# Router in column halves, half of batch 1's convolution on TensorE, and a new order up to routing

## Chip, cores and metric

One core of a Trainium2 chip. The metric is the device time of one execution in microseconds (us). All times below are us unless they say ns.

## What is computed

The input x has 8 batches of 512 tokens with 1024 channels. Each token is convolved along its batch, a router picks one of 8 experts for it, and that expert's 1024 x 1024 matrix is applied. The result is added to x. All of it is float32.

```
y = depthwise causal conv1d(x, taps of cond_2048, K = 8 taps, per channel) + b
idx = argmax_e(y . w_router[e])          # E = 8 experts, one for each token
out = x + w_experts[idx] @ y
```

Tokens are sorted by expert into tiles of 128 rows; 35 tiles have rows, of at most 39 (`NS`).

## The kernel before, in words

**Channels and chunks.** The 1024 channels are 8 chunks (`c`) of 128 partitions. Four chunks are one half (`h`). A unit `u = (b, j0, nj)` is a run of `nj` blocks of 128 tokens of batch `b`. All batches are one unit of four blocks, except batch 2, which is cut in two (`early` is the first of them, (2, 0, 2)), because the list `STAGES` (L37) has a stage that ends after 10 blocks.

**Convolution on VectorE.** One step convolves two chunks of a unit. `first_taps` (L203) makes tap 0 with the bias on ScalarE into a tile of the ring `acc` (three buffers, each one half of a unit); `other_taps` (L220) adds seven taps on VectorE, 14 instructions a step. `begin` (L278) lets ScalarE be up to three steps ahead, as far as `acc` has room.

**Convolution on TensorE.** `spread_taps(c)` (L310) makes eight 128 x 128 diagonal matrices of the taps of a chunk on ScalarE, in slot 0 of the weight buffer `w_all`; `conv_on_pe` (L315) multiplies the shifted rows by them and adds up in PSUM. Before, this is done for chunks 0 to 5 of the early unit.

**Outs.** `conv_out` (L242), here called an out, turns 128 tokens of one half back to rows: four transposes on TensorE into PSUM (`pc`), a copy on ScalarE into `rt`, and after the last block of the unit one DMA on ScalarE's queue to `conv_rows` in DRAM. Only then is the `acc` buffer free.

**Router.** The convolution is linear, so `router_batch` (L352) multiplies x itself by taps times router weights: 64 columns (8 taps x 8 experts), 8 chunks accumulated in PSUM. ScalarE copies the result, a DMA writes it to `z_rows` in DRAM, and SP's queue reads it back shifted by tap into `zs`; `router_logits` (L373) adds the taps by a matmul with `sel`. Batches 0 and 1 are in `xp`, batches 2 to 7 in the three slots of `w_all`, loaded at the start.

**Routing.** L419 to L633 is a chain of small instructions, nearly all on VectorE, with a few matmuls: argmax (`best`, `chosen`), counts by expert (`ps_tot`, `upto`), the place of each token, and last `tok_gather`, `tile_info` and `tile_count`.

**Tiles.** Stage m of `STAGES` says that the first m blocks of 128 tokens are convolved. Each stage makes full tiles for every expert that has 128 rows left, and `last_stage(t)` (L43) is the stage by which tile t surely exists. `fetch(t)` (L706) gathers a tile's rows from `conv_rows` and x on GpSimd's queue; `turn` (L711) transposes them (`cxT`); `multiply` (L724) does 32 passes of 512 columns into `y_ring`; `add_x` (L737) adds x on VectorE; `finish_tile` scatters. `load(t)` (L684) reads an expert's 4.2 MB into one of three slots of `w_all`, in two DMAs on SP's queue, if the expert changes. The slot is a register value. For dependencies, `weights` (L668) treats it as slot `t % 3`. The load of tile 1 waits for the gather of tile 0.

**Order.** The schedule is by hand: what is written first stands first in an engine's queue. Up to routing the order is that of L390 to L406. After it a planner (L753 to L835) keeps two clocks, `now["pe"]` and `now["conv"]`: 1.75 for two chunks of a tile, 0.5 for an out or a turn, 9.4 or 5.4 for a convolution step, 0.7 for an `add_x`, and 14.0 (`LAND`) from a fetch to its turn. It puts a step, an out or a turn where its clock says that it is due. A tile is fetched when `2 * last_stage(t)` outs are written and it is at most two tiles ahead. `load_conv_x(b + 2)` stands where the last step of batch b is.

Of the kernel before, what the change touches and what calls it, by code (L numbers as in the profile page):

```python
# [33 lines left out]
KE = K * E  # L34


STAGES = (8, 10, 12, 16, 20, 24, 32)  # L37
W = len(STAGES)
R = W * E
U = 40  # L40
# [14 lines left out]
def conv_then_routed_ffn(  # L55
# [58 lines left out]
    def iota(shape, pattern, base, channel, name, dtype=F32):  # L114
        t = rc.tile(shape, dtype, name=name)
        nc.gpsimd.iota(
            t,
            pattern=pattern,
            base=base,
            channel_multiplier=channel,  # L120
            allow_small_or_imprecise_dtypes=True,
        )
        return t
# [12 lines left out]
        wr_sb.unsqueeze(2).to_broadcast([P, NC, K, E]),  # L136
        ALU.mult,
    )
    lbw = zp.tile([P, NC, KE], F32, name="lbw")
    nc.vector.memset(lbw, 0.0)  # L140
    nc.vector.tensor_copy(lbw[:, :, KE - E :], wr_sb)

    col = iota([P, P], [[1, P]], 0, 0, "col")
    row = iota([P, 1], [[1, 1]], 0, 1, "row")
# [2 lines left out]
    nc.vector.tensor_tensor(rowu, rowu, row, ALU.add)  # L147
    falling = iota([P, E], [[-1, E]], E, 0, "falling")
    high = iota([P, NT], [[P, NT]], -BIG, 0, "high")
    sel_i = iota([KE, E], [[-1, E]], KE, 1, "sel_i", I32)  # L150
    nc.vector.tensor_single_scalar(sel_i, sel_i, E - 1, op=ALU.bitwise_and)
    sel_f = rc.tile([KE, E], F32, name="sel_f")
    nc.vector.tensor_copy(sel_f, sel_i)
    sel = rc.tile([KE, E], F32, name="sel")
    nc.vector.tensor_single_scalar(sel, sel_f, 0.0, op=ALU.is_equal)
    ones = rc.tile([P, P], BF16, name="ones")
    nc.vector.memset(ones, 1.0)
    notbelow = rc.tile([P, P], BF16, name="notbelow")
# [31 lines left out]
    def operands(u, c):  # L190
# [9 lines left out]

        return acc, shifted

    def first_taps(u, c):  # L203

        b, j0, nj = u
        if c % HC == 0:
            acc_of[u, c // HC] = accp.tile(
                [P, HC, nj * P], F32, tag="acc", name=f"acc_{b}_{j0}_{c // HC}"
            )
        acc, shifted = operands(u, c)  # L210
        for i in (c, c + 1):
            nc.scalar.activation(  # L212
                acc(i),
                shifted(i, 0),
                AF.Identity,
                bias=bias_sb[:, i : i + 1],
                scale=taps_sb[:, i, 0:1],
            )
# [23 lines left out]
    def conv_out(u, h, j):  # L242
# [13 lines left out]
            nc.scalar.dma_start(to.rearrange("(j p) d -> p j d", p=P), rt_of[u, h])  # L256


    ON_PE = 6
    early = next(u for u in units if u[0] == 2)  # L260
    steps = [
        (u, c) for u in units for c in range(0, NC, 2) if u != early or c >= ON_PE
    ]
    now = {"conv": 12.0}
    outs = []
# [12 lines left out]
    def begin():  # L278

        while steps and len(begun) < 3:  # L280
            u, c = steps[0]
            full = [key for key in acc_of if key not in drained]
            if c % HC == 0 and (len(full) >= 3 or u[0] not in xp_of):
                return
            if c % HC and (u, c // HC) not in acc_of:
                return
            first_taps(u, c)
            begun.append(steps.pop(0))
# [3 lines left out]
    def next_step():  # L292
        begin()
        u, c = begun.pop(0)
        other_taps(u, c)
        now["conv"] += 9.4 if u[2] == TB else 5.4
        if c % HC == HC - 2:
            outs.extend((now["conv"] + 1.0, u, c // HC, j) for j in range(u[2]))
        if c == NC - 2 and u[1] + u[2] == TB and u[0] + 2 < B:
            load_conv_x(u[0] + 2, 1)  # L300
        begin()

    def more_steps():
        return bool(steps or begun)

    diag_of = w_all[:, 0].rearrange("p c f -> p (c f)").rearrange(
        "p (c k q) -> p c k q", k=K, q=P
    )

    def spread_taps(c):  # L310

        for k in range(K):
            nc.scalar.mul(diag_of[:, c, k, :], ident, taps_sb[:, c, k : k + 1])

    def conv_on_pe(u, c):  # L315
        b, j0, nj = u
        n = nj * P
        if c % HC == 0:
            acc_of[u, c // HC] = accp.tile(
                [P, HC, n], F32, tag="acc", name=f"acc_{b}_{j0}_{c // HC}"  # L320
            )
        acc, shifted = operands(u, c)
        pc = ps.tile([P, n], F32, tag="pc", name=f"pcv_{b}_{j0}_{c}")
        for k in range(K):
            nc.tensor.matmul(  # L325
                pc, lhsT=diag_of[:, c, k, :], rhs=shifted(c, k), start=(k == 0), stop=(k == K - 1)
            )
        nc.scalar.activation(acc(c), pc, AF.Identity, bias=bias_sb[:, c : c + 1], scale=1.0)
        if c % HC == HC - 1:
            outs.extend((now["conv"], u, c // HC, j) for j in range(nj))  # L330

    ps_lb = psr.tile([KE, 1], F32, tag="pt", name="ps_lb")
    for c in range(NC):
        nc.tensor.matmul(
            ps_lb, lhsT=lbw[:, c, :], rhs=bias_sb[:, c : c + 1], start=(c == 0), stop=(c == NC - 1)
        )
    lb = const.tile([KE, 1], F32, name="lb")
    nc.scalar.copy(lb, ps_lb)  # L340

    lg = psr.tile([P, NT, E], F32, tag="y", name="lg")
# [2 lines left out]
    zs_of = {}  # L345
    zbs = []
    for i in range(2):
        zb = zp.tile([KE, ZL], F32, name=f"zb_{i}")
        nc.gpsimd.memset(zb, 0.0)
        zbs.append(zb)  # L350

    def router_batch(b):  # L352
        pz = ps.tile([KE, S], F32, tag="pc", name=f"pz_{b}")
        for c in range(NC):
            nc.tensor.matmul(  # L355
                pz,
                lhsT=wrt[:, c].rearrange("p k e -> p (k e)"),
                rhs=x_of[b][:, c, :],
                start=(c == 0),
                stop=(c == NC - 1),  # L360
            )
        zb = zbs[b % 2]
        nc.scalar.activation(zb[:, K - 1 : K - 1 + S], pz, AF.Identity, bias=lb, scale=1.0)
        nc.scalar.dma_start(z_rows[b], zb)

        zs = zp.tile([KE, S], F32, tag="zs", name=f"zs_{b}", bufs=B)
        z = z_rows[b]
        nc.sync.dma_start(
            zs, bass.AP(z.tensor, z.offset, [[E * ZL + 1, K], [ZL, E], [1, S]])
        )  # L370
        zs_of[b] = zs

    def router_logits(b):  # L373
        for j in range(TB):
            nc.tensor.matmul(
                lg[:, b * TB + j, :],
                lhsT=zs_of[b][:, j * P : (j + 1) * P],
                rhs=sel,
                start=True,
                stop=True,  # L380
            )

    def some_outs(n):
        for _ in range(n):
            next_out()

    def before_early():
        return steps[0][0] != early or bool(begun)

    for b in range(B):  # L390
        while now["conv"] < 14.0 + 7.0 * b and before_early():
            next_step()
        router_batch(b)
        if b >= 4:
            for c in range(2 * (b - 4), min(2 * (b - 3), ON_PE)):
                spread_taps(c)
        if b == B - 2:
            some_outs(TB)
    for i in range(B - 1):
        router_logits(i)  # L400
    while before_early():
        next_step()
    some_outs(TB)
    router_logits(B - 1)
    some_outs(TB)
    conv_on_pe(early, 0)  # L406
    zp_cm.__exit__(None, None, None)
    rp_cm = tc.tile_pool(name="route", bufs=1)
    rp = rp_cm.__enter__()
# [26 lines left out]
    ps_rank = psr.tile([P, E, NT], F32, tag="pt", name="ps_rank")  # L436
    nc.tensor.matmul(ps_tot, lhsT=ones, rhs=chosen, start=True, stop=True)
    nc.tensor.matmul(ps_rank, lhsT=notbelow, rhs=chosen, start=True, stop=True)
    some_outs(TB)
    conv_on_pe(early, 1)  # L440
    conv_on_pe(early, 2)


    upto = new([P, E, NT], "upto")
# [79 lines left out]
    for q in range(4):  # L524
        ts = slice(q * QT, (q + 1) * QT)
        nc.vector.tensor_tensor(
            in_row[:, ts, :],
            colb.unsqueeze(1).to_broadcast([P, QT, P]),
            part[:, 0, ts].unsqueeze(2).to_broadcast([P, QT, P]),
            ALU.is_equal,  # L530
        )
        for t in range(q * QT, (q + 1) * QT):
            nc.tensor.matmul(
                ps_tok,
                lhsT=in_tile[:, t].rearrange("p a u -> p (a u)"),
                rhs=in_row[:, t],
                start=(t == 0),
                stop=(t == NT - 1),
            )
# [39 lines left out]
    perm = new([P, NS], "perm")  # L579
    nc.vector.tensor_scalar(perm, col[:, :NS], to, None, ALU.is_equal)  # L580

    tok_u = new([2 * U, P], "tok_u")
    nc.vector.tensor_copy(tok_u, ps_tok)
    ps_perm = psr.tile([P, NS], F32, tag="pt", name="ps_perm")
# [46 lines left out]
    nc.vector.tensor_copy(tile_info, info_f[:NS, :])  # L631
    nc.vector.tensor_copy(tok_scatter, tok_f)
    nc.vector.tensor_copy(tile_count, end_run[0:1, W - 1, E - 1 :])  # L633
    for c in range(3, ON_PE):
        conv_on_pe(early, c)
    rp_cm.__exit__(None, None, None)
    psr_cm.__exit__(None, None, None)
    rc_cm.__exit__(None, None, None)
# [29 lines left out]
    def weights(t, slot, *at):  # L668

        a = w_all[(slice(None), ds(slot, 1), *at)]
        fixed = w_all[(slice(None), slice(t % WB, t % WB + 1), *at)]
        return bass.AP(
            a.tensor,
            a.offset,
            a.ap,
            runtime_checks=a.runtime_checks,  # L680
            dep_tracking_offset=fixed.offset,
        )
# [69 lines left out]

    STEP, OUT, LAND = 1.75, 0.5, 14.0  # L753
    now["conv"] += 20.0
    now["pe"] = now["conv"] - 4.0
    ready = {}

    def fetch_ready():
# [9 lines left out]
    def load_ready():  # L768
        ahead = 3 if state["fetched"] else 1
        while state["loaded"] < NS and state["loaded"] < state["tile"] + ahead:  # L770
            load(state["loaded"])
            state["loaded"] += 1

    def try_out():
        if outs and outs[0][0] <= now["pe"]:
# [108 lines left out]
```

## Time and profile before

| | us |
|---|---|
| median of 3 runs (lowest, highest) | 724.84 (724.02, 725.93) |
| the profiled execution | 729.59 |
| its span, first to last instruction | 727.8 |
| TensorE busy in the span | 655.6 |
| VectorE busy | 354.8 |
| ScalarE busy | 147.8 |
| mean granted TensorE clock | 0.951 |

PE is TensorE's matmul, PEld its weight load, DVE is VectorE, ACT is ScalarE, POOL is GpSimd, SP is SyncE; a q after the name means its DMA queue. A row of the timeline has start, length, engine, line, operation, `out<-in`, shape, count, and in brackets how long the engine had been idle and what ended that. Lines are those of the kernel before. DMA queue q1 is the loads of SP, q10 the writes of ScalarE, q0 the gathers and scatters of GpSimd.

### The profile page before, as it was taken

How to read it: one execution, taken by the hardware profiler on the slowest of the kernel's cores; microseconds unless marked ns; L12 is line 12 of the kernel's file. 1: busy time of each engine (PE TensorE's matmuls, PEld its weight loads, DVE VectorE, ACT ScalarE, POOL GpSimd, SP SyncE). 2: the span in 40 equal slices, each digit the busy share in tenths (PEclk: the TensorE clock that was granted, in tenths of full speed). 3: DMA queues.
4: the chain of work that ended last, by engine and by line, in shares of the span. 5: the costliest groups of instructions: out<-in, count | busy, mean ns of one | idle time of the engine just before them, and what ended most of it. 6: DMA issues, size and time to landing. Idle time of an engine off the chain costs nothing. (4 is left out here: it accounts for less than half of the span.)

```text
span 727.8 us, 6970 instructions
## 1 busy us (share of the span) xinstructions
PE 655.6 (90%) x2005; PEld 326.8 (45%) x2005; DVE 354.8 (49%) x610; ACT 147.8 (20%) x266; POOL 110.6 (15%) x131
## 2 busy tenths in 40 slices
PE   6997988679697799899999979999999999999990
PEld 2332866334353455355545434444444444444440
DVE  6997871999799298998990000101010101010100
ACT  4256221522321232233111000000000000000000
POOL 1000001020202211211212023112212221122110
PEclk9998898899899799999999998999999999999996
DMA  8992265989899999799999999998473567296320
GB/s 320 426 357 100 71 234 206 368 285 406 304 425 402 386 402 365 284 427 426 421 426 414 406 377 347 405 374 317 165 301 129 191 262 294 87 381 255 118 88 8
DMA packets 42838, 217.63 MB, mean 299 GB/s; under 512 B 4144, under 2 KB 4144, under 8 KB 35120
## 3 DMA queue, kind: packets, MB, share of 16 engines
q1 hardware_dynamic: 17984, 143.73, 49.4%
q0 software_dynamic: 15696, 55.58, 20.6%
q10 hardware_dynamic: 9120, 17.84, 6.6%
q8 instruction: 20, 0.33, 0.2%
q14 instruction: 18, 0.15, 0.1%
HBM read 224.46 MB, written 36.19 MB: 358 GB/s over the span
## 5 line engine op out<-in xcount | busy, mean ns | idle before, releaser
L729 PE MATMUL y<-w_all,cxT 128*128 x1120 | 506.2, 601 | 5.5 <-DVE xr L739 4.8
L729 PEld LDWEIGHTS y<-w_all,cxT 128*128 128x128 f32 x1120 | 208.1, 193 | 231.8 <-issue 222.7
L231 DVE SCALAR_TENSOR_TENSOR sum<-xp,taps_sb,sum 128x512 f32<-128x512 f32 (+1 forms) x330 | 206.8, 706 | 0.0
L739 DVE TENSOR_TENSOR xr<-y,xr 128x512 f32<-128x512 f32 x70 | 47.9, 688 | 325.9 <-PE y L729 325.9
L716 ACT COPY cxT<-pt 128x512 f32<-128x512 f32 x72 | 42.1, 586 | 357.5 <-PE pt L715 356.4
L715 PE MATMUL pt<-ident,cx 128*128 128x128 f32 x288 | 46.3, 289 | 26.0 <-DMA cx<-conv_rows,tok_gather 26.0
L252 ACT COPY rt<-pc 128x512 f32<-128x512 f32 x64 | 37.1, 585 | 129.1 <-PE pc L247 129.1
L715 PEld LDWEIGHTS pt<-ident,cx 128*128 128x128 f32 x288 | 37.7, 149 | 56.1 <-DMA cx<-conv_rows,tok_gather 28.2
L660 POOL DMA_INDIRECT xr<-in_x,tok_gather x37 | 35.2, 953 | 181.0 <-DMA out<-xr,tok_scatter 176.7
L660 POOL DMA_INDIRECT cx<-conv_rows,tok_gather x37 | 35.8, 968 | 166.0 <-DMA conv_rows<-rt 93.2
L743 POOL DMA_INDIRECT out<-xr,tok_scatter x35 | 36.0, 1029 | 150.4 <-DVE xr L739 134.4
L231 DVE SCALAR_TENSOR_TENSOR sum<-xp,taps_sb,acc 128x512 f32<-128x512 f32 (+1 forms) x66 | 44.1, 711 | 20.9 <-ACT acc L212 20.9
L247 PE MATMUL pc<-ident,acc 128*128 128x128 f32 x256 | 41.5, 293 | 12.5 <-DVE acc L231 6.7
L247 PEld LDWEIGHTS pc<-ident,acc 128*128 128x128 f32 x256 | 33.1, 150 | 39.8 <-issue 24.2
L212 ACT ACTIVATE acc<-xp,bias_sb,taps_sb 128x512 f32<-128x512 f32 (+1 forms) x66 | 46.9, 772 | 6.4 <-ACT rt L252 2.9
L231 DVE SCALAR_TENSOR_TENSOR acc<-xp,taps_sb,sum 128x512 f32<-128x512 f32 (+1 forms) x66 | 43.4, 698 | 0.0
L355 PE MATMUL pz<-w_all,wrt 128*64 128x512 f32 x96 | 42.9, 608 | 0.0
L355 PEld LDWEIGHTS pz<-w_all,wrt 128*64 128x64 f32 x96 | 13.4, 141 | 28.8 <-issue 28.2
L325 PE MATMUL pcv<-xp,w_all 128*128 128x256 f32 x96 | 24.4, 417 | 0.3 <-issue 0.2
L325 PEld LDWEIGHTS pcv<-xp,w_all 128*128 128x128 f32 x96 | 20.0, 211 | 5.8 <-issue 2.2
L92 POOL MEMSET xp<- 128x64 f32 x8 | 1.2, 156 | 104.6 <-DVE acc L231 104.3
L355 PE MATMUL pz<-xp,wrt 128*64 128x512 f32 x32 | 15.4, 642 | 1.3 <-DMA xp<-in_xT 1.3
(106 smaller groups left out, 83.4 us busy)
## 6 DMA issues: line engine op xcount, KB each, us to landing
w_all<-in_w_experts SPq DMA_DIRECT2D x74, 2048.0 KB
xp<-in_xT SPq DMA_DIRECT2D x7, 2048.0 KB
conv_rows<-rt ACTq DMA_DIRECT2D x14, 1024.0 KB
w_all<-in_xT SPq DMA_DIRECT2D x6, 2048.0 KB
xp<-in_xT SPq DMA_DIRECT2D x2, 1024.0 KB
conv_rows<-rt ACTq DMA_DIRECT2D x4, 512.0 KB
z_rows<-zb ACTq DMA_DIRECT2D x8, 130.0 KB
zs<-z_rows SPq DMA_DIRECT2D x8, 128.0 KB
```

Source lines behind the costliest of these rows:

```text
L212: nc.scalar.activation(acc(i), shifted(i, 0), AF.Identity, bias=bias_sb[:, i : i + 1], scale=taps_sb[:, i, 0:1],)
L231: nc.vector.scalar_tensor_tensor(acc(i) if k == K - 1 else sums[i - c], shifted(i, k), taps_sb[:, i, k : k + 1], acc(i) if k == 1 else sum ...
L247: nc.tensor.transpose(pc[:, c * P : (c + 1) * P], acc_of[u, h][:, c, j * P : (j + 1) * P], ident)
L252: nc.scalar.copy(rt_of[u, h][:, j, :], pc)
L325: nc.tensor.matmul(pc, lhsT=diag_of[:, c, k, :], rhs=shifted(c, k), start=(k == 0), stop=(k == K - 1))
L355: nc.tensor.matmul(pz, lhsT=wrt[:, c].rearrange("p k e -> p (k e)"), rhs=x_of[b][:, c, :], start=(c == 0), stop=(c == NC - 1),)
L660: return nc.gpsimd.indirect_dma_start(out=to[:], out_offset=None, in_=src, in_offset=bass.IndirectOffsetOnAxis(ap=tok_gather[:, t : t + 1] ...
L715: nc.tensor.transpose(pt[:, c, :], cx_of[t][:, at * P : (at + 1) * P], ident)
L716: nc.scalar.copy(cxT_of[t][:, h * HC : (h + 1) * HC, :], pt)
L729: nc.tensor.matmul(y_ring[h], lhsT=cxT_of[t][:, c, :], rhs=weights(t, slot_of[t], c, fs).rearrange("p s f -> p (s f)"), start=(c == 0), st ...
L739: nc.vector.tensor_tensor(xr, y_ring[h], xr, ALU.add)
L743: nc.gpsimd.indirect_dma_start(out=out, out_offset=bass.IndirectOffsetOnAxis(ap=tok_scatter[:, t : t + 1], axis=0), in_=xr_of[t][:], in_of ...
```

## The change

The router takes two batches at a time: `router_pair(g)` puts the 64 columns of batch 2g on partitions 0 to 63 of one PSUM tile and those of batch 2g + 1 on 64 to 127, chunk by chunk in turn. The z tiles, `lbw`, `sel` and `lb` have twice the rows, and a logit matmul gives both batches. The second half of batch 1 (chunks 4 to 7, `second`) is convolved on TensorE, with the diagonals of chunks 4 and 5 in a buffer of `rt`; of the early unit, TensorE does chunks 0 to 3 and VectorE two steps instead of one. `conv_on_pe` is a generator that gives one tap at a time, so that its taps can stand between other matmuls. The order up to routing is written out; seven of the outs of batch 1 and the early unit's chunks stand after routing. The stage at 20 blocks is gone. Dependencies of a weight load are tracked one slot further on. The load of x for batch 3 stands behind the weight load of tile 1. The planner starts `now["pe"]` at `now["conv"]`.

```diff
-STAGES = (8, 10, 12, 16, 20, 24, 32)
+STAGES = (8, 10, 12, 16, 24, 32)
...
-    lbw = zp.tile([P, NC, KE], F32, name="lbw")
+    lbw = zp.tile([P, NC, 2 * KE], F32, name="lbw")
     nc.vector.memset(lbw, 0.0)
-    nc.vector.tensor_copy(lbw[:, :, KE - E :], wr_sb)
+    for i in (1, 2):
+        nc.vector.tensor_copy(lbw[:, :, i * KE - E : i * KE], wr_sb)
...
-    ON_PE = 6
+    second = next(u for u in units if u[0] == 1)
     early = next(u for u in units if u[0] == 2)
+    on_pe = {second: range(HC, NC), early: range(HC)}
     steps = [
-        (u, c) for u in units for c in range(0, NC, 2) if u != early or c >= ON_PE
+        (u, c) for u in units for c in range(0, NC, 2) if c not in on_pe.get(u, ())
     ]
...
+    diag_rows = rows.tile([P, 2, K, P], F32, tag="rt", name="diag_rows")
...
+    def diag(c):
+        return diag_rows[:, c - HC] if c in (HC, HC + 1) else diag_w[:, c]
...
+    def run(work, n=K):
+        for _ in range(n):
+            next(work)
...
+    def router_pair(g):
+        pz = ps.tile([2 * KE, S], F32, tag="pc", name=f"pz_{g}")
         for c in range(NC):
+            for i in range(2):
+                nc.tensor.matmul(
+                    pz[halves[i]],
+                    lhsT=wrt[:, c].rearrange("p k e -> p (k e)"),
+                    rhs=x_of[2 * g + i][:, c, :],
+                    start=(c == 0),
+                    stop=(c == NC - 1),
+                )
...
-    for b in range(B):
-        while now["conv"] < 14.0 + 7.0 * b and before_early():
-            next_step()
-        router_batch(b)
-        if b >= 4:
-            for c in range(2 * (b - 4), min(2 * (b - 3), ON_PE)):
-                spread_taps(c)
-        if b == B - 2:
-            some_outs(TB)
-    for i in range(B - 1):
-        router_logits(i)
-    while before_early():
-        next_step()
+    first = next(u for u in units if u[0] == 0)
+    for h in range(2):
+        new_acc(first, h)
+    new_acc(second, 1)
+    pe = {c: conv_on_pe(second, c) for c in on_pe[second]}
+    spread_taps(HC)
+    next_step()
+    router_pair(0)
+    next_step()
+    spread_taps(HC + 1)
+    run(pe[HC])
+    router_pair(1)
     some_outs(TB)
-    router_logits(B - 1)
+    next_step()
+    run(pe[HC + 1])
+    spread_taps(HC + 2)
+    router_pair(2)
+    next_step()
+    spread_taps(HC + 3)
+    router_pair(3)
+    next_step()
     some_outs(TB)
-    conv_on_pe(early, 0)
+    for c in range(HC):
+        spread_taps(c)
+    next_step()
+    begin()
+    for g in range(B // 2):
+        router_logits(g)
+        if g == B // 2 - 2:
+            run(pe[HC + 2], 3)
+    run(pe[HC + 2], 1)
...
-    some_outs(TB)
-    conv_on_pe(early, 1)
-    conv_on_pe(early, 2)
+    run(pe[HC + 2], 4)
...
+        if q == 0:
+            run(pe[HC + 3], 4)
+        else:
+            run(pe[HC + 3], 1)
...
+    run(pe[HC + 3], 1)
+    some_outs(1)
     tok_u = new([2 * U, P], "tok_u")
...
-    for c in range(3, ON_PE):
-        conv_on_pe(early, c)
+    some_outs(2 * TB - 1)
+    new_acc(early, 0)
+    begin()
+    for c in on_pe[early]:
+        run(conv_on_pe(early, c))
...
-        fixed = w_all[(slice(None), slice(t % WB, t % WB + 1), *at)]
+        i = (t + 1) % WB
+        fixed = w_all[(slice(None), slice(i, i + 1), *at)]
...
-    now["pe"] = now["conv"] - 4.0
+    now["pe"] = now["conv"]
...
             state["loaded"] += 1
+            if state["loaded"] == 2:
+                load_conv_x(second[0] + 2, 1)
```

## The prediction

> **What bounds the kernel now.** I first cut the span into stages, at times that the timeline gives: start of the routing chain (87.20), its last instruction (112.06), first expert matmul (136.09), start of tile 9 (315.4), start of tile 17 (447.7). The columns are busy time of PE, PEld, DVE, ACT and POOL, then granted clock, DMA share and GB/s.
>
> ```profile
> 0.00:87.20 87.20, 75.84 (x242) 34.35 (x243) 77.12 (x129) 37.41 (x82) 2.86 (x18) 0.92 0.66 254
> 87.20:112.06 24.86, 19.29 (x120) 15.79 (x119) 18.98 (x60) 5.87 (x11) 0.00 (x0) 0.95 0.60 212
> 112.06:136.09 24.03, 17.05 (x71) 13.86 (x70) 9.05 (x25) 9.38 (x19) 2.04 (x2) 0.78 0.81 299
> 136.09:315.40 179.31, 152.96 (x472) 77.08 (x473) 156.99 (x259) 49.28 (x78) 29.73 (x33) 0.93 0.93 364
> 315.40:447.70 132.30, 127.25 (x386) 62.41 (x385) 67.11 (x103) 24.80 (x41) 24.46 (x25) 0.97 0.99 404
> 447.70:711.00 263.30, 263.19 (x721) 123.33 (x719) 24.95 (x37) 21.06 (x36) 50.46 (x52) 1.00 0.64 244
> ```
>
> The last stage is pure TensorE: 18 tiles of 14.61. So the end is set by when tile 0 starts and by what PE loses until tile 17: 26.4 idle before tile 9 and 5.1 after it. Next the timeline up to routing:
>
> ```profile
> 7.92 15.36 PE L355 MATMUL pz<-xp,wrt 128*64 128x512 f32 x32 [1.26 <-DMA xp<-in_xT]
> 15.88 0.13 PEld L355 LDWEIGHTS pz<-xp,wrt 128*64 128x64 f32 x1 [0.36 <-DMA xp<-in_xT]
> 16.25 0.14 PEld L355 LDWEIGHTS pz<-xp,wrt 128*64 128x64 f32 x1 [0.23 <-issue]
> 16.67 0.14 PEld L355 LDWEIGHTS pz<-xp,wrt 128*64 128x64 f32 x1 [0.29 <-issue]
> ...
> 66.06 8.43 PE L355 MATMUL pz<-w_all,wrt 128*64 128x512 f32 x16
> 74.42 7.92 PE L375 MATMUL lg<-sel,zs 64*128 64x8 f32 x56
> 85.27 1.40 DVE L231 SCALAR_TENSOR_TENSOR acc<-xp,taps_sb,sum 128x512 f32<-128x512 f32 x2
> 87.20 0.43 DVE L420 TENSOR_REDUCE best<-lg 128x32 f32<-128x256 f32 x1 [0.54 <-POOL xp L92]
> 93.50 0.69 DVE L445 TENSOR_TENSOR_SCAN upto<-carry,ps_tot 128x256 f32<-128x256 f32 x1 [4.04 <-PE ps_tot L437]
> ```
>
> Every matmul appears as two passes. A router pass comes every 0.43, its load of 0.14 lies beside the pass before; a batch is 16 passes, 6.87. Routing waits for VectorE's eighth convolution step (9.22 each) and for the router, about equally late. Then tile 0, and tile 5 as the pattern of a stage's first tile:
>
> ```profile
> 112.06 0.13 DVE L633 CAST tile_count<-end_run 1x1 int32<-1x1 f32 x1
> 127.18 0.98 DVE L231 SCALAR_TENSOR_TENSOR sum<-xp,taps_sb,acc 128x256 f32<-128x256 f32 x2 [14.98 <-ACT acc L212]
> 132.52 1.72 PE L247 MATMUL pc<-ident,acc 128*128 128x128 f32 x6 [6.71 <-DVE acc L231]
> 136.09 7.61 PE L729 MATMUL y<-w_all,cxT 128*128 x16
> ...
> 218.00 0.36 ACTq L256 DMA_DIRECT2D conv_rows<-rt  x1
> 231.41 0.98 POOL L660 DMA_INDIRECT cx<-conv_rows,tok_gather  x1 [28.18 <-PE y L729]
> 241.69 1.97 PE L715 MATMUL pt<-ident,cx 128*128 128x128 f32 x8 [10.17 <-DMA cx<-conv_rows,tok_gather]
> ```
>
> From the write of a stage's last rows to the turn of its first tile: 23.7. The DMA view of 217 to 226 (packets, MB) says why: the write on q10 crawls beside the weights on q1.
>
> ```profile
> q1 hardware_dynamic: 236, 3.60, 95.2%
> q10 hardware_dynamic: 101, 0.21, 5.9%
> ```
>
> **The change, up to routing.** VectorE does six steps instead of eight: 6 x 9.22 = 55.3. It starts later than 8.83: `lbw` doubles (its memset 0.48 to about 0.9, one copy of 0.20 more) and puts `lb` at 7.3; then `spread_taps` (16 in 4.78, so 2.4 for eight) stands ahead of the first taps on ScalarE. Start 10.7, end 66.0. The doubled `sel` costs some 0.3 inside that delay. ScalarE makes 64 diagonals instead of 48 (+4.8), but was busy for 37.4 of the 87.2 and nothing waits for them that early; the first two chunks' diagonals take one of the two `rt` buffers, and the second half of batch 0 that needs it is turned after they are read: nothing for both.
>
> TensorE becomes the later one. No trace shows two column halves. From below: fully side by side, a pair of batches is 6.87. From above: one after the other, 13.7. The Trainium skill (TensorE: Matmul & The Clock Gate, Part 3) says that a weight load overlaps running matmuls only where the row groups differ; the halves share theirs, so by the rule 32 x 0.14 would come on top, 18.2 a pair, and the change would lose. The rows at 16.25 and 16.67 show such loads inside the 0.43 pitch with all rows in use, so I take the trace. The same part gives 2.38x for three column tiles, an efficiency of 0.79, by estimate 8.7 a pair. I take 7.4, near the full overlap. The sum: batch 1 is there at 15.9; 4 pairs 29.7; two convolved chunks (16 passes each, 512 columns) 13.7; eight outs at 0.63 (four took 2.50 at 93.40) 5.0; logits of three pairs, 24 passes x 0.141, 3.4; three taps of the third chunk 2.6; last logits 1.1. Routing starts at 71.4 + 0.5 = 72.0, 15.2 earlier. The last pair ends at 61.8; its way through DRAM (0.7 on ScalarE, 2.25 from write to read issue, about as much back) is over by 68, ahead of the last logits at 70.3. The loads of x are not moved, and batch 7 must only be there by 54; SP's new order (xp 2 ahead of the last `zs`) costs nothing while VectorE frees that buffer, at 48, before the last pair ends at 61.8.
>
> **Routing.** The wait of 4.04 shrinks to 0.3, since a single tap stands ahead on PE instead of four outs and a chunk. One DVE operation fewer, -0.15. Taps between the `ps_tok` matmuls: 0.86 + 0.61 a quarter against DVE's 1.15, +0.6. So 24.86 becomes 21.7 and the chain ends at 93.7, 18.4 earlier.
>
> **Tile 0.** Before, its weights waited for the diagonals in slot 0 and its turn for a VectorE step that began 15 late. Both go: dependencies are now tracked one slot on, and steps c4 and c6 of the early unit run right after routing (11.0, done at 105). What is late next: seven of batch 1's outs run only now (92.4 to 96.9) and their last write, 1 MB, is issued at 97.9, behind 4.2 MB of weights issued at 96.1. The skill (DMA: Bandwidth & Descriptors, Queues, rings and completion order) has an engine alternate between queues by packets. Equal shares of bytes would give the write 5 us; but the packets above are 15.3 and 2.1 KB, 12% by that rule and less in the trace. I take the trace: weights gone at 107.6, write at 109.5, `cx` 5 later, turned in 2.2: first matmul at 117.2. PE's own work (ps_run, seven outs, 4 chunks x 3.45, four outs) ends at 112.4 and is hidden; without the crawl tile 0 starts at 114.6. Gain so far 18.9.
>
> **Tiles 0 to 9.** I followed the planner's arithmetic (L753 to L835) through both versions. PE work is 9 x 14.61 + 32 outs x 0.43 = 145.3 (before 28 outs, 143.5); the remainder of 152.9 that was not idle, 9 us, is slow clock after idle, of which I keep 8. Idle:
> - Tile 1: xp 3, loaded at 86.82 before, is now queued on SP behind tile 1's weights, which wait for tile 0's gather. ScalarE's first taps of batch 3 wait for it, and tile 1's `cxT` copies stand behind them. 8.3 MB with the gathers at 0.4 from 115.5 end at 136.3, copies at 138.4; tile 1 was due at 135.5: 3. That load's memset (0.15) and the third load's wait for the diagonals in slot 0 (read by 112) hold up nothing.
> - Tile 3: between 0 and the 7.2 of before; its write now leaves some 15 ahead of the turn instead of 17, but with one load fewer in front (the third is no load, tile 2 has tile 1's expert, and tile 3's starts 8 ahead of the write): 3. Tile 5: its write leaves 2.2 into tile 4, so 12.3 of tile 4 and four outs (1.7) cover 14.0 of the 23.7, which leaves 9.7; if no new load runs into the gather as at 231, some 17 in all and 3. I take 7 (10.2 before).
> - Tile 9: stage 20 is gone, so it needs all 48 outs of batches 0 to 5. The planner puts the last two out after tile 8 and plans a wait of 14.0. Real: write 2 after tile 8's end, behind that tile's slot being reloaded; 22 to the turn (23.7 at tile 5), less four useful outs: 18.
>
> Together 145.3 + 8 + 31 = 184.3 against 179.3: 5.0 given back.
>
> **After tile 9.** Four outs fewer (1.7) and about 1 of waiting for `add_x`: -2.7. Counting the reference's routing by each stage list, the weights are loaded 25 times instead of 27, 8.4 MB less. PE never waited for `w_all`; a load (4.2 MB, 10.5 us at 0.4) hides under a tile, so this is worth nothing.
>
> Sum: -18.9 + 5.0 - 2.7 = -16.6. The profiled execution took 729.59 (span 727.8 and 1.8 around) and would take 713.0. The median of the runs, 724.84, is 4.75 lower; with the same difference it becomes 708.2.
>
> **Rivals.**
> - A: as summed, 708; with 8 either way for the bounds of tiles 5 and 9 and of the pair, 700 to 716. 0.55.
> - B: the halves overlap and the writes do not crawl, since fewer weights are under way: tile 0 at 114.6 (2.6), tile 5 without a wait (7), tile 9 with 8 (10): 19.6 less, 688.6, and up to 700 where only some of it comes. For it: the shortest landing of a write was 4.4. Against it: 0.93 to 0.99 DMA share up to tile 17. 0.15.
> - C: the wait for tile 9 doubles, because xp 7 waits on SP for VectorE and holds a weight load behind it (they were issued at 296.75 and 299.58): 716 to 726. 0.14, of which 0.04 within 0.3%, about what a measurement can tell from no change.
> - D, slower: the halves run one after the other. Each pair takes 13.7, 25.3 more in all on the path to routing, and nothing hides it, as VectorE is done at 66: 733.5. It decides from 11.6 a pair on, where the 16.6 are spent; with exposed loads (18.2) it is 751. For it: no row shows an overlap; against it: the three-tile figure. With a ScalarE stall that I did not see, 0.16.
>
> So faster 0.80, same 0.04, slower 0.16. From 688 to 728 leaves out D and a tail.
>
> **What would show it.** Right: `pz` records of two halves starting together, a pair in 7 to 8.7; `best` near 72; last routing cast near 94; tile 0 at 115 to 119; an idle of 15 to 22 ahead of tile 9's turn; 14.61 a tile at the end. Wrong: pairs of 13.7, or `upto` still waiting for PE; a wait of ScalarE on xp 3 well beyond 138; a tile 9 that waits over 30.

## The result and the profile after

| | before | after |
|---|---|---|
| median of the runs, us | 725.38 (724.02 to 729.56, 4 runs) | 743.65 (743.22 to 744.86, 4 runs) |
| ratio, 95% interval | 1 | 1.0245 [1.0201, 1.0288] |
| profiled execution, us (span) | 729.59 (727.8) | 744.86 (743.1) |

The kernel became slower by 18.3 us, where 16.6 less were forecast; 743.65 lies above the range of 688 to 728. Of the rivals only D, priced at 733.5 and with exposed loads at 751, is near it, and what D names, halves that run one after the other, did not happen. A few runs fell into a slower state of the chip and are left out of every ratio; three of the medians below (xp 3 alone, the halves in turn, xp 2 in after) still count one each. The profiled execution of before is some 4 above its median, that of after 1.2, so the two profiles differ by only 15.3. A position compared between the two traces is uncertain by the 3 us between 18.3 and 15.3: after and the first seven of its variants below run the same code up to routing, and in their eight profiles routing starts at 75.81 to 78.77.

The table cuts the execution at the same places in both traces and beside the forecast: the first routing instruction (`best`), the last routing cast, the first expert matmul of tile 0, of tile 9 and of tile 17, and the last matmul. Behind that lie 18.7 us in both profiles.

| stretch, us | before | predicted | after | after less predicted |
|---|---|---|---|---|
| up to routing | 87.2 | 72.0 | 77.8 | +5.8 |
| routing | 24.9 | 21.7 | 21.5 | -0.2 |
| to tile 0 | 24.0 | 23.5 | 30.3 | +6.8 |
| tiles 0 to 9 | 179.3 | 184.3 | 206.1 | +21.8 |
| tile 9 to the last matmul | 395.5 | 392.8 | 390.5 | -2.3 |

Three of these stretches in the windows view of after; the columns are the window, its length, then busy time and instructions of TensorE, its weight loads, VectorE, ScalarE and GpSimd, the granted clock, the DMA share and GB/s:

```profile
0.00:77.81 77.81, 64.45 (x247) 28.67 (x248) 59.52 (x105) 32.62 (x73) 2.69 (x17) 0.96 0.76 298
...
99.26:129.55 30.29, 23.32 (x109) 19.49 (x109) 25.54 (x66) 11.56 (x23) 2.21 (x3) 0.84 0.79 282
129.55:335.60 206.05, 156.68 (x490) 79.57 (x489) 166.45 (x262) 54.31 (x86) 29.62 (x33) 0.86 0.92 362
```

From tile 9 on TensorE is busy nearly without a gap (387.0 of 390.5). The loss is in the last row shown: TensorE is busy for 156.7 of 206.1, at a clock of 0.86, while DMA is at its busiest (0.92). What it waits for is mostly transfers. First the way to routing, in the timeline of after (start, duration, instruction, idle time ahead of it and what ended that):

```profile
32.47 7.09 PE L375 MATMUL pz<-w_all,wrt 128*64 128x512 f32 x32
...
64.54 0.33 ACTq L385 DMA_DIRECT2D z_rows<-zb  x1
...
69.70 5.47 PE L335 MATMUL pcv<-xp,w_all 128*128 128x512 f32 x6
71.25 1.20 SPq L389 DMA_DIRECT2D zs<-z_rows  x2
76.58 1.03 PE L398 MATMUL lg<-sel,zs 128*128 128x16 f32 x8 [1.41 <-DMA zs<-z_rows]
...
77.81 0.42 DVE L455 TENSOR_REDUCE best<-lg 128x32 f32<-128x256 f32 x1 [9.96 <-PE lg L398]
```

Thirty-two passes over two halves end in 7.09 where sixteen over one half took 6.87: the halves run side by side. The last pair's rows are written from 64.54 and read from 71.25 on. VectorE waits 9.96 for TensorE's logits, so TensorE is now the later one, as forecast; `upto`, not shown, waits 0.51 instead of 4.04. The logits wait 1.41 for the z rows. Then tiles 0 and 1:

```profile
105.43 0.37 ACTq L263 DMA_DIRECT2D conv_rows<-rt  x1
121.56 1.10 POOL L702 DMA_INDIRECT cx<-conv_rows,tok_gather  x1 [71.81 <-DVE sum L238]
129.11 0.60 SPq L96 DMA_DIRECT2D xp<-in_xT  x1
129.55 10.78 PE L772 MATMUL y<-w_all,cxT 128*128 x20
...
153.99 2.93 ACT L219 ACTIVATE acc<-xp,bias_sb,taps_sb 128x512 f32<-128x512 f32 x4 [23.64 <-DMA xp<-in_xT]
160.35 5.16 PE L772 MATMUL y<-w_all,cxT 128*128 x7 [13.11 <-ACT cxT L759]
```

The gather of tile 0 comes 16.1 after the issue of the write that it reads. TensorE starts tile 0 at 129.55. The load of xp 3 is issued at 129.11; ScalarE stands 23.64 for it, with tile 1's `cxT` copies behind, and TensorE 13.11 for those. Tile 1 starts at 160.35, no earlier than before (159.9). And tiles 5 and 9:

```profile
213.09 0.37 ACTq L263 DMA_DIRECT2D conv_rows<-rt  x1
...
234.84 0.99 POOL L702 DMA_INDIRECT cx<-conv_rows,tok_gather  x1 [34.95 <-DMA conv_rows<-rt]
...
308.05 0.37 ACTq L263 DMA_DIRECT2D conv_rows<-rt  x1
314.31 0.47 PE L254 MATMUL pc<-ident,acc 128*128 128x128 f32 x1 [6.29 <-DVE acc L238]
329.41 0.98 POOL L702 DMA_INDIRECT cx<-conv_rows,tok_gather  x1 [32.03 <-issue]
333.81 1.97 PE L758 MATMUL pt<-ident,cx 128*128 128x128 f32 x8 [15.81 <-DMA cx<-conv_rows,tok_gather]
```

Tile 5's rows take 21.8 from write to gather, and TensorE waits 11.80 for them (not shown). The idle time ahead of tile 9 is 22.5: TensorE waits 6.29 for VectorE's step for the next outs, which stand ahead of the turn, and 15.81 for the gathered rows, with smaller gaps. Both lie within the 25.8 from the write at 308.05 to the turn, so it is the rows that end the wait. The row of the gather names "issue", which tells nothing. The write at 308.05, 21.4 ahead of it, is the 14th, by the list of stages the last that tile 9 reads. Tile 8 to tile 9 takes 43.9, before 18.2.

### The profile page after: what moved, and what is told of

Read it like the earlier page. It is cut to its first block, busy times and chain, and to the rows that moved or that the text cites. A ratio compares the mean times of both kernels' runs of the same rounds, so it can differ in the third digit from the quotient of the medians.

```text
span 743.1 us, 6969 instructions
## 1 busy us (share of the span) xinstructions
PE 649.4 (87%) x2005; PEld 320.3 (43%) x2005; DVE 342.9 (46%) x598; ACT 148.4 (20%) x278; POOL 110.6 (15%) x131
## 3 DMA queue, kind: packets, MB, share of 16 engines
q1 hardware_dynamic: 17408, 135.34, 46.2%
## 5 line engine op out<-in xcount | busy, mean ns | idle before, releaser
L772 PE MATMUL y<-w_all,cxT 128*128 x1120 | 504.1, 600 | 17.1 <-ACT cxT L759 13.1
L238 DVE SCALAR_TENSOR_TENSOR sum<-xp,taps_sb,sum 128x512 f32<-128x512 f32 (+1 forms) x320 | 197.5, 697 | 0.0
L238 DVE SCALAR_TENSOR_TENSOR sum<-xp,taps_sb,acc 128x512 f32<-128x512 f32 (+1 forms) x64 | 42.2, 701 | 24.7 <-ACT acc L219 24.7
L219 ACT ACTIVATE acc<-xp,bias_sb,taps_sb 128x512 f32<-128x512 f32 (+1 forms) x64 | 45.0, 765 | 34.5 <-DMA xp<-in_xT 25.2
L238 DVE SCALAR_TENSOR_TENSOR acc<-xp,taps_sb,sum 128x512 f32<-128x512 f32 (+1 forms) x64 | 41.5, 688 | 0.0
L335 PE MATMUL pcv<-xp,w_all 128*128 128x256 f32 (+1 forms) x96 | 35.3, 522 | 0.0
L375 PE MATMUL pz<-w_all,wrt 128*64 128x512 f32 x96 | 21.0, 594 | 0.0
L375 PE MATMUL pz<-xp,wrt 128*64 128x512 f32 x32 | 11.4, 788 | 5.0 <-DMA xp<-in_xT 5.0
L335 PE MATMUL pcv<-xp,diag_rows 128*128 128x512 f32 x32 | 14.3, 598 | 0.2 <-ACT rt L259 0.2
L326 ACT ACTIVATE w_all<-ident,taps_sb 128x128 f32<-128x128 f32 x48 | 14.3, 387 | 0.4 <-ACT zb L383 0.4
```

Source lines behind the costliest of these rows:

```text
L219: nc.scalar.activation(acc(i), shifted(i, 0), AF.Identity, bias=bias_sb[:, i : i + 1], scale=taps_sb[:, i, 0:1],)
L238: nc.vector.scalar_tensor_tensor(acc(i) if k == K - 1 else sums[i - c], shifted(i, k), taps_sb[:, i, k : k + 1], acc(i) if k == 1 else sum ...
L335: nc.tensor.matmul(pc, lhsT=diag(c)[:, k, :], rhs=shifted(c, k), start=(k == 0), stop=(k == K - 1))
L375: nc.tensor.matmul(pz[halves[i]], lhsT=wrt[:, c].rearrange("p k e -> p (k e)"), rhs=x_of[2 * g + i][:, c, :], start=(c == 0), stop=(c == N ...
L772: nc.tensor.matmul(y_ring[h], lhsT=cxT_of[t][:, c, :], rhs=weights(t, slot_of[t], c, fs).rearrange("p s f -> p (s f)"), start=(c == 0), st ...
```

## Experiments

The theory after this reading: the start is gained in part; the removed stage at 20 costs tile 9 more than that; the rest is lost to row writes that crawl beside queued weights, and to xp 3. The rivals: the waits only move when one is taken away; the crawl, not the order of the stages, makes tile 9's wait; the reordered start is the loss. Each ratio is against runs of before on the same chip, whose medians were 724.3 to 726.1.

**Stage 20 put back**, in after and, as its mirror, taken out of before.

```
-STAGES = (8, 10, 12, 16, 24, 32)
+STAGES = (8, 10, 12, 16, 20, 24, 32)
```

> The changed kernel with one edit: the stage at 20 blocks is back in the list of stages. Theory (three separate waits): the 22.5 us of idle in the step of tile 8 fall to under 5, the weights are loaded twice more at no cost, and the time is 722 to 729. Rival (what is late is the convolution itself): tile 9 no longer waits but tile 13 does for the same rows, 737 to 743.

Measured: 717.86, ratio to before 0.9899 [0.9843, 0.9954], 25.8 less than after and below the range that was expected.

> The kernel before with one edit: the stage at 20 blocks is taken out of the list of stages. Theory (the missing stage costs by itself): a wait of 12 to 22 us appears ahead of tile 9, 735 to 745. Rival (it costs only beside the new order, where VectorE's steps and TensorE's outs stand elsewhere): within 4 us of the kernel before, since two weight loads fewer pay for it.

Measured: 752.5, ratio 1.0353 [1.0281, 1.0424], 28.2 more than before and above the range that was expected. The turn of tile 9 in TensorE's timeline, in after with the stage:

```profile
293.84 0.60 PE L758 MATMUL pt<-ident,cx 128*128 128x128 f32 x4
294.28 3.60 PE L772 MATMUL y<-w_all,cxT 128*128 x8
```

The same in before without the stage, with GpSimd's gather:

```profile
335.72 0.99 POOL L660 DMA_INDIRECT cx<-conv_rows,tok_gather  x1 [31.63 <-DMA conv_rows<-rt]
...
339.92 1.97 PE L715 MATMUL pt<-ident,cx 128*128 128x128 f32 x8 [13.88 <-DMA cx<-conv_rows,tok_gather]
```

With the stage the turns stand among tile 8's matmuls with no wait, and tile 8 to 9 takes 15.9 instead of 43.9. Without it the old order shows what the new one does: 13.88 for the gather, 39.7 from tile 8 to 9 instead of 18.2. So the stage alone is worth 25 to 28 us in either order, by the ratios and by the medians. With it the change is faster than before by 1.0%; only small gaps came up behind it (1.42 and 3.47; tile 17 starts at 434.7, before 447.7).

**xp 3 ahead of tile 0's weights**, alone and with the stage.

```
     run(pe[HC + 3], 1)
+    load_conv_x(second[0] + 2, 1)
...
             state["loaded"] += 1
-            if state["loaded"] == 2:
-                load_conv_x(second[0] + 2, 1)
```

> The changed kernel with one edit: the load of x for batch 3 stands on SP's queue ahead of tile 0's weights instead of behind tile 1's. Theory (the loss is three separate waits: ScalarE on this load at tile 1, tile 9 on the missing stage, tile 0 on rows that crawl behind weights): the 13.1 us of idle ahead of tile 1 shrink to under 3, tile 9 starts 9 to 13 earlier, and the time is 730 to 735. Rival (what is late is the convolution itself, so that a wait taken away comes back at the next stage's first tile): the waits ahead of tiles 5 and 9 grow by as much as tile 1's shrinks, 740 to 744.

Measured: 737.76, 1.0161 [1.0087, 1.0235]. Tile 1's wait is gone and tile 1 starts 14.5 earlier, but tile 3, without a wait in after, now waits 9.53, so tile 9 starts only 8.4 earlier. The gather of tile 3 in this kernel; the write that it reads was issued at 152.67:

```profile
169.79 0.96 POOL L703 DMA_INDIRECT cx<-conv_rows,tok_gather  x1 [20.33 <-DMA conv_rows<-rt]
```

17.1 lie between the two: the time won at tile 1 arrives where the next rows aren't in DRAM yet. Of the 13 that were taken away, some 6 are left at the end: the theory had the wait right, the rival the part that is given back.

> The changed kernel with two edits: the stage at 20 blocks is back, and x for batch 3 is loaded ahead of tile 0's weights. Theory as it stands now (ScalarE's stall at tile 1 goes, but the rows of later stages crawl behind the weights that then come closer together): tile 3 waits 9 as it did with the second edit alone, and the time is 709 to 714, 4 to 9 under the stage alone (717.9). Rival (the stall at tile 1 is worth its full 12): 703 to 707.

Measured: 714.29, 0.9862 [0.9832, 0.9892]; tile 3 waits 9.12 and tile 5 11.7. On top of the stage xp 3 is worth 2.7 by the ratios, which their intervals don't tell from nothing.

**Tile 0's weights only after its gather.** This takes the weights out of the write's way.

```
-            if t == 1 and h == 0:
+            if t <= 1 and h == 0:
...
-        ahead = 3 if state["fetched"] else 1
+        ahead = 3 if state["fetched"] else 0
```

> The changed kernel with one edit: tile 0's weights also wait for the gather of tile 0's rows, as tile 1's do, so that batch 1's last rows are written with no weights in front. Theory (three separate waits): the gather of tile 0 is issued near 109 instead of 121.6, tile 0 starts at 121 to 127 instead of 129.5, x for batch 3 lands 5 to 10 earlier, 731 to 739. Rival (the rows wait for the engines, not for the queue): the gather is issued as late as before and tile 0 starts later by the length of its weight load, 10 us: 750 or more.

Measured: 745.76, 1.0279 [1.0222, 1.0337]: no gain, against the expectation. ScalarE's queue and GpSimd in its timeline, the first write and the gathers of tiles 0 and 1:

```profile
103.75 0.37 ACTq L263 DMA_DIRECT2D conv_rows<-rt  x1
```

```profile
110.36 1.12 POOL L702 DMA_INDIRECT cx<-conv_rows,tok_gather  x1 [60.88 <-DVE sum L238]
...
143.05 0.94 POOL L702 DMA_INDIRECT cx<-conv_rows,tok_gather  x1 [30.16 <-DMA conv_rows<-rt]
```

With no weights beside it the first write is read 6.6 later instead of 16.1: the crawl is real and costs tile 0's gather 9.5 us. But the weights follow, TensorE waits 4.05 for them, the next rows (write issued at 123.34) crawl behind them for 19.7, and waits of 8.64 and 6.93 come up at tiles 1 and 3. The write was sped up and the loads weren't made fewer; the wait moved.

**Weights in small packets.** A half of an expert's weights is loaded as four DMAs of one chunk instead of one of four, so eight DMAs an expert. That makes the packets smaller; it may also let each chunk be loaded as soon as that chunk's place is free, and no run separates the two.

```
-        for h in range(2):
-            cs = slice(h * HC, (h + 1) * HC)
+        for h in range(NC):
+            cs = slice(h, h + 1)
```

> The changed kernel with only the weights in eight DMAs of one chunk. Theory (tile 9's wait is the way of its rows through DRAM, and most of that is the write behind the weights): the gather of tile 9 follows its write by 8 to 14 instead of 21.4, the 15.8 ahead of its turn shrink to 3 to 8, and with tiles 0 and 5 the time is 718 to 730. Rival (tile 9 waits because of the order, VectorE's steps and the outs in front of its turn): its idle stays above 18, 735 or more.

Measured, in after: 723.83, 0.9964 [0.9939, 0.9989], 19.8 less than after. The queues (packets, MB, share) in 8 us behind the write that tile 9 reads, in after and then with small packets; q1 carries the weights, q10 the rows:

```profile
q1 hardware_dynamic: 224, 3.15, 91.9%
q10 hardware_dynamic: 143, 0.29, 9.4%
```

```profile
q1 hardware_dynamic: 692, 2.52, 77.6%
q10 hardware_dynamic: 381, 0.78, 25.2%
```

A weight packet shrank from 14.1 to 3.6 KB, a row packet stayed at 2.05, and the rows' part of the bytes went from 8% to 24%. In both, the write gets about 0.6 packets for each of the weights': the Trainium skill (DMA: Bandwidth & Descriptors, Queues, rings and completion order) has the engines alternate between queues by packets, which would make that 1 if its packets are those that the profile counts; by that count the rule has the direction and not quite the size. Tile 9 in this kernel; the write that it reads was issued at 291.11:

```profile
303.74 0.98 POOL L702 DMA_INDIRECT cx<-conv_rows,tok_gather  x1 [23.29 <-DMA conv_rows<-rt]
```

```profile
312.66 1.97 PE L758 MATMUL pt<-ident,cx 128*128 128x128 f32 x8 [11.50 <-DMA cx<-conv_rows,tok_gather]
```

From write to gather 12.6 instead of 21.4, but from gather to turn 8.9 instead of 4.4. TensorE still waits 11.50, and 6.29 for VectorE ahead of that, where 3 to 8 were expected for the gather. So smaller packets take about 4 off tile 9's wait; 18 stay, for the order (the rows are made too late) and for the way through DRAM, which is still slower than the 6.6 without weights. Tile 1 has no wait and tile 5 one of 5.2 instead of 11.8. Tile 0 gains nothing: its gather comes 14.0 after its write instead of 16.1, but TensorE then waits 8.55 for ScalarE and starts it at 133.31, 3.8 later than in after (routing starts 1.0 later in this profile).

> The kernel before with only the weights in eight DMAs of one chunk. Theory (weights in large packets starve the rows there too): the idle ahead of tiles 1, 3 and 5 falls from 22.4 to 5 to 12, 708 to 717. Rival (the DMA engines are full, whatever the packets): within 3 of the kernel before.

Measured, in before: 716.83, 0.9883 [0.9854, 0.9912]. The waits for gathered rows at tiles 1, 3 and 5 fall from 22.4 to 4.4; of these 18 about half is left at the end, as other waits of 2 to 3 come up at tiles 1, 2 and 3. The crawl was a loss of the old kernel too.

> The changed kernel with the stage at 20 blocks back and each expert's weights loaded in eight DMAs of one chunk instead of two of four, so that a partition's piece is 4 KB instead of 16 KB. Theory (a row write gets its turn by packets, and 16 KB packets of weights starve it): the rows' write behind weights lands in 5 to 9 us instead of 13 to 17, tile 0 starts 5 to 8 earlier, tile 5 waits under 6 instead of 12.2, 700 to 711. Rival (the DMA engines are full, whatever the packets): a write takes as long as before, and the time stays within 3 of 717.9.

Measured, with stage 20 in the new order: 702.48, 0.9689 [0.967, 0.9708], 3.1% under before and, by the medians, 5.5% under after. The time is as expected, the way there is not: tile 0, expected 5 to 8 earlier, starts at 131.85 instead of 126.99.

> The changed kernel with all three edits: the stage at 20 blocks is back, x for batch 3 is loaded ahead of tile 0's weights, and the weights come in eight DMAs of one chunk. Theory (ScalarE's stall, now 7.7 ahead of tile 0 and 0.8 ahead of tile 1 with the stage and the small packets, goes, and the rows get their turn): 692 to 698. Rival (with ScalarE free the rows of tiles 3 and 5 come back as waits, as in the run of stage and x alone): 699 to 703, no better than stage and small packets.

Measured, with xp 3 first as well: 705.43, 0.9732 [0.9706, 0.9759]: nothing more, as the rival said, and even above its range. ScalarE in this kernel:

```profile
129.50 0.37 ACTq L263 DMA_DIRECT2D conv_rows<-rt  x1
130.04 1.07 ACT L760 COPY cxT<-pt 128x512 f32<-128x512 f32 x2 [8.14 <-DMA w_all<-in_w_experts]
```

The last rows are copied by 121.90, their write is issued 7.6 later, and the copies that tile 0 needs stand behind it (TensorE waits 7.25). Every kernel with small packets in the new order shows such a stand. The trace puts its end down to a weight DMA here, and to VectorE in another of them, and the write depends on neither; why the issue stood is not settled.

**The halves one after the other**, with stage 20: the loops over `i` and `c` swapped.

```
-        for c in range(NC):
-            for i in range(2):
+        for i in range(2):
+            for c in range(NC):
```

> The changed kernel with the stage at 20 blocks back and the two halves of a router pair one after the other (all chunks of one batch, then all of the other), with the same instructions. Theory (side by side they save 6.9 a pair on the path to routing, and nothing hides it): pairs of 13.7, routing 24 to 28 later, 738 to 746 against 717.9. Rival (part of it is hidden, since VectorE and the rows of later stages get ahead meanwhile): 722 to 735.

Measured: 729.38, 1.0077 [1.0047, 1.0106], 11.5 more by the medians (12.9 by the ratios) than with the halves alternating. The two pairs ahead of routing, alternating and then in turn:

```profile
49.73 13.95 PE L375 MATMUL pz<-w_all,wrt 128*64 128x512 f32 x64
```

```profile
52.46 22.70 PE L375 MATMUL pz<-w_all,wrt 128*64 128x512 f32 x64
```

A pair takes 11.35 instead of 6.97, 17.5 over four pairs. Routing begins 9.7 later, tile 0 9.8 and tile 17 8.1: some 8 are hidden, as the rival said. Alternating the halves is worth 11 to 13 by medians and ratios, and the two profiles differ by 8.0. That a pair in turn takes 11.35, and not the 13.7 of two batches by themselves, is seen in its single records: the four halves of the second view begin at 52.46, 57.67, 62.87 and 68.08, so that the first four passes of a half run beside the last four of the half before it.

**xp 2 behind the last pair's reads**, in after and in the fastest kernel. It tries the prediction's "SP's new order ... costs nothing".

```
         if c == NC - 2 and u[1] + u[2] == TB and u[0] + 2 < B:
-            load_conv_x(u[0] + 2, 1)
+            if u[0] > 0:
+                load_conv_x(u[0] + 2, 1)
...
     router_pair(3)
+    load_conv_x(2, 1)
```

> The changed kernel with one move: the load of xp 2 (2 MB) is issued behind the last pair's reads of the z rows, where the changed kernel issues it ahead of them. Theory: the last pair's way through DRAM (0.26 MB) took 6.7 from write to read issue because the 2 MB were under way beside it; without them about 2.3 to 3, so that the last logits wait for nothing and routing starts at 76 to 76.5 instead of 77.8. The taps of chunk 6 stay slow, since that window's granted clock was 0.50. The gain at the end is at most 1.5, as tile 1 and tile 9 wait for other things: 741 to 744. Rival: ScalarE's or SP's own order makes the delay, and the read is issued 6 or more behind the write again, with routing at 77.8; or batch 2's convolution comes later by it and costs VectorE steps before tile 1: 744 to 748.

Measured: 742.82, 1.0229 [1.0187, 1.0272], an interval that largely overlaps that of after.

> The same move in the fastest kernel so far (stage 20 kept, weights in small packets, 702.5). Theory: routing 1 to 1.5 earlier, and since ScalarE's write ahead of tile 0 is what its first tile waits for, 0 to 1.5 at the end: 701 to 702.5. Rival: xp 2 comes later and delays VectorE's steps behind routing, 703 to 706.

Measured: 699.55, 0.9643 [0.9608, 0.9679], the lowest of all, though its interval touches that of the kernel it was made from. The last logits, first in that kernel without the move, then with it:

```profile
75.15 1.86 PE L398 MATMUL lg<-sel,zs 128*128 128x16 f32 x8 [3.99 <-DMA zs<-z_rows]
```

```profile
69.34 5.45 PE L336 MATMUL pcv<-xp,w_all 128*128 128x512 f32 x6
74.60 0.98 PE L399 MATMUL lg<-sel,zs 128*128 128x16 f32 x8
```

The wait of 3.99 is gone and the logits follow the taps. The read is issued 2.05 after the write (2.06 in after with the move); in the eight profiles with xp 2 ahead and the same code up to routing it is 5.6 to 6.9. So xp 2's 2 MB beside the z rows delayed their read, as the theory said. The start of routing shows less of it: 75.77, where the eight have 75.81 to 78.77, 77.2 in the mean. One reason is the clock: the six taps took 2.82 at a granted clock of 1.00 in the one and 5.45 at 0.52 in the other. The move need not be what slowed it: among the eight profiles of the same code the six taps take 2.82 in four and 4.31 to 5.47 in the other four. At the end the move is worth 0 to 3.

## Why the prediction was wrong

**Right.** The pair: 7.4 predicted, 6.97 measured, near full overlap; the records of the two halves start within 0.01 of each other. The rule of the Trainium skill that the prediction weighed at 18.2 and set aside, that loads overlap only with other row groups (TensorE: Matmul & The Clock Gate, Part 3), does not hold here. Routing itself: 21.7 against 21.5, with `upto` freed. TensorE as the later one ahead of routing. Two loads of weights fewer worth nothing: before lost 25 to 28 with its stage removed, though q1 then moved 135.34 MB instead of 143.73. After tile 9: -2.7 predicted, -5.0 measured. Rival D, the slower one, had the halves wrong, and its price of 25.3 "and nothing hides it" was too high as well: the halves in turn cost 11.5. But the "ScalarE stall that I did not see", which it also allows for, is what came at tile 1. So did a sign of being wrong, "a wait of ScalarE on xp 3 well beyond 138": it ended at 153.99. The other sign, a tile 9 that waits over 30, did not come.

**Routing starts 5.8 later than forecast.** "Its way through DRAM ... is over by 68" failed: the last pair ended at 63.7 (61.8 predicted), its rows were written from 64.54, but read only at 71.25, 6.7 later instead of 2.25, and were used at 76.58. With xp 2 moved behind that read it is issued 2.05 after the write, so "SP's new order ... costs nothing" was wrong: not the buffer's wait but the 2 MB on the way beside the rows were the price. The three taps took 5.47 instead of 2.6 at a granted clock of 0.50, beside the wait for the rows, so of these two only the later one counts. With the rows in time routing still starts at 75.77, 3.8 later than forecast, as the taps took 5.45 there too; in after the rows cost the 1.41 that the logits wait beyond the taps.

**"First matmul at 117.2" was 129.55**, 12.4 later: routing ended 5.6 later, the last outs took 2.0 more, the write needed 16.1 to its gather instead of 11.6, and the rest 0.3 more. Of the 18.9 that should have been gained here 6.5 were. The crawl as such was right, since with the weights held back the gather comes 6.6 after the write; its size was off by 4.5.

**"Tile 1 ... 3" was 13.1.** The chain was named correctly (xp 3 behind tile 1's weights behind the gather, ScalarE behind xp 3, the copies behind ScalarE). Its sizes were not. That tile 0 came late explains none of it: the gather was 12.1 later than forecast, but tile 1 was also due 11.7 later (147.2 instead of 135.5). From the gather to ScalarE's start lie 32.4 (121.56 to 153.99), where 26.8 were counted (109.5 to 136.3): the way through the queue took 5.6 longer. And from there to tile 1's matmuls lie 6.4 instead of 2.1, as six first taps, two copies of rows and a write stand ahead of tile 1's copies on ScalarE. Moving that load took all of the 13 away, and some 6 of it were left at the end.

**Tiles 5 and 9.** "I take 18" was 22.5: from write to turn 25.8 passed where 22 were taken, and four outs covered 3.5 of it. "I take 7" at tile 5, between two cases, was 11.8: its rows (written at 213.09, gathered at 234.84) took 21.8 to the gather, against 13.4 in the old trace. Tile 3 was 0 instead of 3. The four waits are 47.4 where 31 were forecast. Of the other 5.4 of this stretch, 3.4 are slower passes (156.7 busy where 145.3 + 8 were counted, at a clock of 0.86 instead of the 0.93 of before) and 2.0 small gaps.

**The step that failed.** In the sum "-18.9 + 5.0 - 2.7" the mechanisms were right but for xp 2 beside the z rows and the clock of the taps, and the sizes of the first two terms were wrong. In the profiles the start paid 6.5 instead of 18.9: 5.6 of the 12.4 are the late routing (the last pair 1.9 later, then the slow taps and the z rows beside xp 2), 4.5 the write behind the weights and 2.0 the outs. From tile 0 to tile 9 26.7 were given back instead of 5.0: 10.1 at tile 1, 4.8 at tile 5, 4.5 at tile 9, less 3 at tile 3, and the 5.4 above. The removed stage, charged with 18, costs 25 to 28 in both orders. Correcting any one of these would still have left a forecast of a gain; together they turn the sign. With the stage kept the same change is at 717.86, under before.

## What to carry to other kernels

When a change removes a stage at which produced rows are consumed early, ask first what the stage was buying: here it let VectorE's steps, a DRAM write and a gather run beside a tile's matmuls, and fewer weight loads, hidden anyway, were no return for it. A saving at the start only counts if the next thing that is consumed is ready that much earlier too; for each wait behind it, count all that stands in front on the queue and on the engine, as the bytes ahead of xp 3 and ScalarE's own work did here. Where a small latency-critical write shares DMA engines with bulk loads, try the bulk loads in smaller pieces before reordering anything: it took 8 to 9 us off the old kernel and 15 to 20 off the new one, though tile 0 gained nothing by it.

## What was not expected of the hardware

- Two matmuls on the two halves of TensorE's columns, over the same rows, ran side by side when they were issued alternately: 32 passes in 6.97 against 11.35 with the halves one after the other, where only four passes of each half lay beside the next.
- A write of 2 KB packets got 8% of the bytes beside loads of 14 KB packets and 24% beside 3.6 KB packets.
- ScalarE's issue of a write stood for 7.6 with its data ready while many loads were under way; its cause is open.
- The same six passes of taps ahead of routing took 2.82 in four executions and 4.31 to 5.47 in four others of the same code; the granted clock was 1.00 in the first four and 0.50 to 0.65 in the others. What made the clock fall was not tried.
